# An attention block gated by an fp4 feed-forward on one core: another order of the first 90 microseconds

## The chip, the cores and the metric

The kernel runs on one core of one Trainium2 chip, as one launch. The metric is the device time of that core in microseconds. The five engines of the core run their own instruction streams in order: TensorE (matmuls and transposes), VectorE, ScalarE, GpSimd, and SyncE, which issues most of the DMAs. They wait for each other by semaphores.

## The reference, cut to what matters

The input `x` is 4 x 2048 x 256 in float32. It is normalized over the last axis, and the normalized tokens go two ways: through an attention without softmax (whose sums over all tokens reduce to the Gram matrix of the normalized tokens), and through a feed-forward of width 704 whose three products have both operands quantized to fp4 in blocks of 16.

```python
def fp4_quant_dequant(x):                    # blocks of 16 along the last axis
    scale = jnp.maximum(jnp.max(jnp.abs(xb), axis=-1, keepdims=True) / 6.0, 1e-12)
    xn = xb / scale
    q = _GRID[jnp.searchsorted(_MID, jnp.abs(xn))] * jnp.sign(xn) * scale
...
    h = jax.nn.silu(fp4_linear(x, w_gate)) * fp4_linear(x, w_up)
    return fp4_linear(h, w_down)
...
    xn = _layernorm(x, axis=-1)              # mean, variance, eps 1e-5
    s = attention(xn, Wq, bq, Wk, bk, Wv, bv, gamma)   # x + gamma * weight_value
    g = _silu(ffn(xn, w_gate, w_up, w_down))
    return x + s * g
```

The attention of a batch of 2048 tokens needs all tokens of that batch before any of its output can be made; the feed-forward of a group of tokens needs only that group and the weights.

## The kernel before, in words

The 8192 tokens are cut into 32 groups of 256, eight groups to a batch; a group is a tile of 128 partitions by two tokens by 256. Each group passes these stages, each a function of the kernel:

- `load_x`: the DMA of the tokens, issued by SyncE.
- `statistics` (lines 269 to 284): mean and variance by VectorE (`bn_stats`, `bn_aggr`), and two integer operations that start an inverse square root. `deviations` (286 to 298) ends that root by three Newton steps of four tiny operations each on GpSimd (`inv_sqrt_steps`, line 258) and makes `rstd` and `shift`.
- `normalize` (300): two ScalarE activations write the normalized tokens `xn`.
- `gram_step` (316): TensorE adds the group to the Gram matrix; `turn_xn` (336) transposes the group, evicted by ScalarE.
- `scale_x` (352) and `rounded` (229): the quantization to fp4. VectorE finds the largest of each block (line 151), its inverse (160, 162) and the quotient (177); ScalarE shortens it to 16 bits (`short`, 205); five VectorE operations round it to the grid and multiply by the scale (222 to 226, 235).
- `turn_xq` (360): TensorE transposes the quantized group, ScalarE evicts it.
- `gate_up` (436): a piece of the first two products: one of the group's two token halves with one of three chunks of the gate and up weights. ScalarE evicts it as `si` and `up`, GpSimd multiplies these to `h`. `pieces(n, i)` issues both halves of group n with chunk i.
- `scale_h`, `turn_q`, `rescale_h`: the quantization of `h`, with its transpose by DMA and its scales spread through memory. `down` (464) is the last product.

The weights pass the same quantization once: `scale_gu` (705) scales one of the three chunks (the quotient of chunks 1 and 2 is made by GpSimd, line 197), `turn_gu` transposes it, and `wd`, `turn_d` do the same for `w_down`, in six parts that a generator yields.

The order of instructions on each engine is the order in which these functions are called: the tile framework is put in a manual schedule and adds only the semaphores. Lines 776 to 879 are the front, a list of calls written out by hand, which quantizes the weights and brings groups 0 to 3 through gate and up and groups 4 to 6 partly; behind it a loop (893 to 966) handles one group per turn, with the steps of attention as a generator in between. `keep_busy` (496) issues matmuls of zeros whose result nobody reads.

PSUM buffers matter for the order: transposes rotate through two banks (`ps_tp`), gate-up pieces through two (`ps_gu`), so each needs ScalarE's eviction of the one before the last.

Of the kernel before, what the change touches and what calls it, by code (L numbers as in the profile page):

```python
# [15 lines left out]
LN_EPS = 1e-5  # L16
# [8 lines left out]
def kernel(  # L25
# [124 lines left out]
    def largest(sc: bass.AP, src: bass.AP):  # L150
        nc.vector.tensor_reduce(  # L151
            sc, src.rearrange("p a (n k) -> p a n k", k=BLK), AX.X, ALU.max, apply_absolute_value=True
        )
# [30 lines left out]
        )  # L184
        return sc, y, F, kind, nm

    def scaled(src: bass.AP, F: int, kind: str, nm: str, multiplier=nc.vector):
        n, a = F // BLK, src.shape[1]
        most = T * L if kind == "x" else HF
        sc = small.tile([P, most // BLK], F32, tag="scx" if kind == "x" else "sch", name=f"sc_{nm}")[:, 0:n]  # L190
        largest(sc, src)
        inv = inverse(sc, nm)
        if multiplier is nc.vector:
            return over(src, inv, F, kind, nm, sc)
        nc.vector.tensor_scalar(inv, inv, DOWN, None, ALU.mult)
        y = tok.tile([P, most], F32, tag="hqt", name=f"y_{nm}", bufs=2)[:, 0:F]
        multiplier.tensor_tensor(
            y.rearrange("p (a n k) -> p a n k", a=a, k=BLK),
            src.rearrange("p a (n k) -> p a n k", k=BLK),
            inv.rearrange("p (a n) -> p a n", a=a).unsqueeze(3).to_broadcast([P, a, n // a, BLK]),  # L200
            ALU.mult,
        )
        return sc, y, F, kind, nm

    def short(state):
        sc, y, F, kind, nm = state
        most = T * L if kind == "x" else HF
        t = tok.tile([P, most], F16, tag="tx" if kind == "x" else "th", name=f"t_{nm}", bufs=2)[:, 0:F]
        upper = y.bitcast(BF16).rearrange("p (f two) -> p f two", two=2)[:, :, 1]
        nc.scalar.activation(t, upper, AF.Copy, scale=1.0 + 2.0**-9)  # L210
        return t
# [17 lines left out]
    def rounded(state, t, multiplier=nc.vector) -> bass.AP:  # L229

        return rescaled(state, on_grid(state, t), multiplier)
# [16 lines left out]
    def inv_sqrt_first(v: bass.AP, nm: str):  # L248
        shape = list(v.shape)
        y = small.tile(shape, F32, tag=f"isq_y{shape}", name=f"isq_y_{nm}")  # L250
        r = small.tile(shape, F32, tag=f"isq_r{shape}", name=f"isq_r_{nm}")
        nc.vector.tensor_scalar(y.bitcast(I32), v.bitcast(I32), 1, None, ALU.logical_shift_right)
        nc.vector.tensor_scalar(
            y.bitcast(I32), y.bitcast(I32), -1.0, float(0x5F3759DF), ALU.mult, ALU.add
        )
        return y, r
# [12 lines left out]
    def statistics(*ns: int):  # L269

        ns = [n for n in ns if n < N]
        if not ns:
            return
        K = T * len(ns)
        mv = small.tile([P, 3 * T, 2], F32, tag="mv", name=f"mv_{ns[0]}")[:, 0:K, :]
        st = small.tile([P, 3 * T, 6], F32, tag="bn", name=f"bn_{ns[0]}", bufs=2)[:, 0:K, :]
        for i, n in enumerate(ns):
            for t in range(T):
                nc.vector.bn_stats(st[:, i * T + t, :], x_sb[n][:, t, :])
        for i in range(K):  # L280
            nc.vector.bn_aggr(mv[:, i, :], st[:, i, :])
        ve = small.tile([P, 3 * T], F32, tag="ve", name=f"ve_{ns[0]}", bufs=2)[:, 0:K]
        nc.vector.tensor_scalar(ve, mv[:, :, 1], LN_EPS, None, ALU.add)
        return ns, mv, ve, inv_sqrt_first(ve, f"ln{ns[0]}")

    def deviations(state):
        if state is None:
            return
        ns, mv, ve, first = state
        K = T * len(ns)  # L290
        rstd = small.tile([P, 3 * T], F32, tag="rstd", name=f"rstd_{ns[0]}")[:, 0:K]
        shift = small.tile([P, 3 * T], F32, tag="shift", name=f"shift_{ns[0]}")[:, 0:K]
        nc.gpsimd.tensor_scalar(shift, mv[:, :, 0], -1.0, None, ALU.mult)
        inv_sqrt_steps(rstd, ve, *first)
        nc.gpsimd.tensor_tensor(shift, shift, rstd, ALU.mult)  # L295
        for i, n in enumerate(ns):
            part = slice(i * T, (i + 1) * T)
            stats[n] = rstd[:, part], shift[:, part]

    def normalize(n: int):  # L300
        if n >= N:
            return
        rstd, shift = stats.pop(n)
        for t in range(T):
            nc.scalar.activation(  # L305
                xns[n % len(xns)][:, t, 0:L],
                x_sb[n][:, t, :],
                AF.Identity,
                scale=rstd[:, t : t + 1],
                bias=shift[:, t : t + 1],  # L310
            )
# [4 lines left out]
    def gram_step(n: int):  # L316

        if n >= N:
            return
        b, g = divmod(n, NG)  # L320
        if g == 0:
            grams[b] = ps_gr.tile([P, 512], F32, tag="gram", name=f"gram_{b}")
        xn = xns[n % len(xns)]

        for t in range(T):
            for c, o in ((0, 0), (1, L + 1)):
                nc.tensor.matmul(  # L327
                    grams[b][:, o : o + L + 1 - c * P],
                    xn[:, t, c * P : (c + 1) * P],
                    xn[:, t, c * P : L + 1],  # L330
                    start=(g == 0 and t == 0 and c == 0),
                    stop=(g == NG - 1 and t == T - 1),
                    skip_group_check=True,
                )
# [161 lines left out]
    def keep_busy(count: int):  # L496

        for _ in range(count):
            nc.tensor.matmul(opened["at"], zero[:, 0:P], zero, start=True, stop=True)

    def preset(n: int, pool=ps_at, tag: str = "at"):
        m_b = whole[n // NG][1]
        ready[n] = pool.tile([P, T, L], F32, tag=tag, name=f"at_{n}")
        nc.scalar.copy(ready[n], m_b.unsqueeze(1).to_broadcast([P, T, L]))
# [197 lines left out]

    wgu = const.tile([P, KC, NB * P], F32, tag="wgu", name="wgu")

    def scale_gu(i: int, multiplier):
        nb = chunks[i][1]
        return scaled(wgu_n[i][:, 0 : nb * L].unsqueeze(1), nb * L, "w", f"gu{i}", multiplier)

    def turn_gu(i: int, wz):
        j0, nb = chunks[i]  # L710
# [65 lines left out]
    open_bank(ps_at, "at")  # L776
    deviations(statistics(0))
    w0 = scale_gu(0, nc.vector)
    normalize(0)
    tw = short(w0)  # L780
    moments = statistics(1)
    s_x = scale_x(0)
    deviations(moments)
    tx = short(s_x)
    gram_step(0)
    turn_xn(0)
    keep_busy(9)
    wz = rounded(w0, tw)
    normalize(1)
    xz = rounded(s_x, tx)  # L790
    turn_gu(0, wz)
    turn_xq(0, xz)
    w1 = scale_gu(1, nc.gpsimd)
    s_x = scale_x(1)
    moments = statistics(2)
    gate_up(0, 0, *chunks[0])
    tx = short(s_x)
    tw = short(w1)
    gate_up(0, 1, *chunks[0])
    deviations(moments)  # L800
    gram_step(1)
    turn_xn(1)
    keep_busy(5)
    turn_xq(1, rounded(s_x, tx))
    w2 = scale_gu(2, nc.gpsimd)
    pieces(1, 0)
    wz = rounded(w1, tw)
    normalize(2)
    tw = short(w2)
    turn_gu(1, wz)  # L810
    moments = statistics(3)
    s_x = scale_x(2)
    deviations(moments)
    tx = short(s_x)
    gram_step(2)
    turn_xn(2)
    pieces(0, 1)
    wz = rounded(w2, tw)
    normalize(3)
    pieces(1, 1)  # L820
    turn_xq(2, rounded(s_x, tx))
    s_x = scale_x(3)
    tx = short(s_x)
    moments = statistics(4, 5, 6)
    pieces(2, 0)
    gram_step(3)
    turn_xn(3)
    xz = rounded(s_x, tx)
    deviations(moments)
    turn_gu(2, wz)  # L830
    wd = scaled(wd_n.unsqueeze(1), HF, "w", "d")
    pieces(2, 1)
    normalize(4)
    pieces(0, 2)
    td = short(wd)
    turn_xq(3, xz)
    s_x = scale_x(4)
    tx = short(s_x)
    pieces(1, 2)
    wdz = rounded(wd, td)  # L840
    turn_qk()
    wd_turns = turn_d(wdz)
    pieces(2, 2)
    load_x(7)
    load_x(8)
    h_state = scale_h(0)
    normalize(5)
    gate_up(3, 0, *chunks[0])
    next(wd_turns)
    gate_up(3, 1, *chunks[0])  # L850
    th = short(h_state)
    next(wd_turns)
    gram_step(4)
    turn_xn(4)
    turn_scales(0)
    turn_xq(4, rounded(s_x, tx))
    turn_q("h", 0, on_grid(h_state, th))
    gate_up(3, 0, *chunks[1])
    next(wd_turns)
    gate_up(3, 1, *chunks[1])  # L860
    next(wd_turns)
    h_state = 1, scale_h(1, 5)
    th = short(h_state[1])
    spread_biases()
    gate_up(3, 0, *chunks[2])
    next(wd_turns)
    gate_up(3, 1, *chunks[2])
    next(wd_turns)
    gram_step(5)
    s_x = scale_x_of(5, 1)  # L870
    tx = short(s_x)
# [188 lines left out]
```

## Time and profile before

| | |
|---|---|
| Median of 3 runs | 667.43 us (665.45 to 667.47) |
| Profiled execution | 666.58 us, span from first to last instruction 664.8 us |
| Busy in the span | PE 639.3 us, PEld 435.3, DVE 528.7, ACT 286.6, POOL 320.5 |
| Mean granted TensorE clock | 0.997 |
| First gate-up matmul of group 0 | 20.27 us |
| First gate-up matmul of group 4 (the loop) | 85.19 us |
| First gate-up matmul of group 5 | 101.68 us |

PE is TensorE's matmuls, PEld its weight loads (which overlap them), DVE is VectorE, ACT ScalarE, POOL GpSimd, SP SyncE. In a line of the timeline the first number is the start in us from the beginning of the span, the second the time to the end of the last of the instructions merged in it; then engine, line of the kernel, operation, output and input tiles with their shape, the count, and in brackets how long the engine had stood idle and what released it. In a list of waits the columns are: the operation that waited and the one that it waited for, total us, times, longest us. The chain that ended last is followed back from the last instruction to whatever released each step.

### The profile page before, as it was taken

Reading aid. Unit: us, or ns where it says so; the run is one execution under the profiler, and the core shown is the slowest. Engines: PE = TensorE matmul, PEld = TensorE weight load, DVE = VectorE, ACT = ScalarE, POOL = GpSimd, SP = SyncE. Lnnn points to the kernel's source line nnn. Section 1 sums busy time; section 2 is a strip of 40 time slices with the busy share of each in tenths; the row PEclk is TensorE's granted clock in tenths of the full one; section 3 lists DMA queues with packets and bytes.
Section 4 is the critical chain, followed back from the end, with each engine's and each line's share of the span. In section 5 each row is a group of like instructions: output and inputs, shape, how many; then the busy total and the mean of one; then the engine's idle time right before and its main releaser. Section 6 shows DMA issues by size and latency. Waiting matters only on the chain.

```text
span 664.8 us, 8117 instructions
## 1 busy us (share of the span) xinstructions
PE 639.3 (96%) x2486; PEld 435.3 (65%) x2486; DVE 528.7 (80%) x911; ACT 286.6 (43%) x701; POOL 320.5 (48%) x545
## 2 busy tenths in 40 slices
PE   3799999999999999999999999999999999999997
PEld 2446556656766666767666666766676666666886
DVE  6998997879866887867969786885997777888752
ACT  2366654344444444344453444444344444433230
POOL 5567445271635526264463636256263736537122
PEclk9999999999999999999999999999999999999999
DMA  9200488857489777764877888749778757884882
GB/s 228 77 17 0 54 101 138 117 53 85 103 122 140 140 115 108 127 99 119 137 112 101 135 125 130 120 121 141 84 113 126 111 113 114 120 125 72 150 176 97
DMA packets 86232, 74.19 MB, mean 112 GB/s; under 512 B 64076, under 2 KB 70444, under 8 KB 86188
## 3 DMA queue, kind: packets, MB, share of 16 engines
q1 hardware_dynamic: 85916, 73.40, 68.3%
q8 instruction: 20, 0.33, 0.2%
q10 hardware_dynamic: 272, 0.26, 0.1%
q14 instruction: 24, 0.20, 0.1%
HBM read 48.30 MB, written 10.27 MB: 88 GB/s over the span
## 4 chain that ended last, share of the span: by engine, by line
PE 83%; DVE 6%; POOL 3%; DMA 3%; ACT 2%; issue 1%; SPq 0%; DVEq 0%; ACTq 0%; POOLq 0%
PE gu L442 40%; PE dn L469 23%; PE at L511 8%; PE gram L327 5%; PE px L575 2%; PE tp_xn L344 2%; PE pm L661 1%; DMA qt_x<-t_x 1%; DMA wv_sb<-in_L_attn_Wv_dram 1%; DMA wgu_n<-in_L_ffn_w_gate_dram 1%; PE pa L640 1%; DMA x<-in_L_attn_x_dram 1%; POOL isq_r_ln L262 1%; PE tp_sc L396 0%; POOL h L455 0%
## 5 line engine op out<-in xcount | busy, mean ns | idle before, releaser
L442 PE MATMUL gu<-wgu,xqt 128*128 128x512 f32 (+1 forms) x768 | 315.9, 560 | 2.2 <-ACT xqt L314 2.2
L455 POOL TENSOR_TENSOR h<-si,up 128x256 f32<-128x256 f32 (+1 forms) x192 | 163.2, 857 | 274.4 <-ACT up L453 274.1
L442 PEld LDWEIGHTS gu<-wgu,xqt 128*128 128x128 f32 x768 | 143.0, 191 | 135.4 <-issue 105.4
L469 PE MATMUL dn<-wdt,hqt 128*128 128x256 f32 x768 | 171.0, 379 | 0.0
L469 PEld LDWEIGHTS dn<-wdt,hqt 128*128 128x128 f32 x768 | 144.2, 190 | 18.9
L451 ACT ACTIVATE si<-gu 128x256 f32<-128x256 f32 (+1 forms) x192 | 70.2, 366 | 192.2 <-PE gu L442 187.4
L419 DVE TENSOR_TENSOR xqt<-qt_x,se 128x512 f32<-128x512 bf16 x27 | 26.0, 961 | 72.0 <-DMA qt_x<-t_x 67.3
L453 ACT COPY up<-gu 128x256 f32<-128x256 f32 (+1 forms) x192 | 67.7, 353 | 0.0
L327 PEld LDWEIGHTS gram<-xn 128*128 128x128 f32 x256 | 44.0, 194 | 27.6 <-ACT xn L305 11.4
L511 PE MATMUL at<-M,xnt 128*128 128x256 f32 x256 | 59.7, 379 | 0.0
L429 DVE TENSOR_TENSOR hqt<-qt_h,se 128x1408 f32<-128x1408 bf16 x32 | 53.8, 1680 | 7.0 <-DMA qt_h<-t_h 7.0
L327 PE MATMUL gram<-xn 128*128 128x257 f32 (+1 forms) x256 | 48.9, 335 | 9.2 <-ACT xn L305 9.2
L177 DVE SCALAR_TENSOR_TENSOR y_h<-h,inv_h 128x1408 f32<-128x1408 f32 x32 | 54.7, 1711 | 2.5 <-ACT t_h L210 1.4
L210 ACT ACTIVATE t_h<-y_h 128x1408 f16<-128x1408 bf16 x32 | 44.3, 1385 | 17.5 <-DVE y_h L177 17.5
L151 DVE TENSOR_REDUCE scs<-h 128x88 f32<-128x1408 f32 x32 | 51.6, 1612 | 0.0
L511 PEld LDWEIGHTS at<-M,xnt 128*128 128x128 f32 x256 | 46.7, 190 | 6.7
L314 ACT COPY sct<-tp_sc 120x128 f32<-120x128 f32 (+1 forms) x32 | 8.4, 265 | 92.7 <-PE tp_sc L396 92.7
L305 ACT ACTIVATE xn<-x,shift,rstd 128x256 f32<-128x256 f32 x64 | 35.0, 597 | 28.2 <-POOL shift L295 28.2
L528 POOL TENSOR_TENSOR gate<-gate,xl 128x512 f32<-128x512 f32 x26 | 35.6, 1370 | 22.4 <-DVE gate L521 22.4
L225 DVE TENSOR_TENSOR t_h<-m_h,t_h 128x1408 bf16<-128x1408 bf16 x32 | 31.1, 972 | 1.1
L226 DVE TENSOR_TENSOR t_h<-t_h,m_h 128x1408 bf16<-128x1408 bf16 x32 | 28.5, 892 | 1.1
L164 DVE RECIPROCAL inv_h<-scs 128x120 f32<-128x120 f32 (+1 forms) x32 | 27.9, 873 | 1.1
(145 smaller groups left out, 662.9 us busy)
## 6 DMA issues: line engine op xcount, KB each, us to landing
se<-there SPq DMA_DIRECT2D x27, 960.0 KB
x<-in_L_attn_x_dram SPq DMA_DIRECT2D x32, 256.0 KB
out_dram<-gate SPq DMA_DIRECT2D x31, 256.0 KB
xl<-in_L_attn_x_dram SPq DMA_DIRECT2D x26, 256.0 KB
se<-there SPq DMA_DIRECT2D x5, 704.0 KB
there<-sct SPq DMA_DIRECT2D x27, 60.0 KB
wd_n<-in_L_ffn_w_down_dram SPq DMA_DIRECT2D x1, 704.0 KB
wgu_n<-in_L_ffn_w_up_dram SPq DMA_DIRECT2D x2, 256.0 KB
```

The costliest lines, as they stand in the source:

```text
L151: nc.vector.tensor_reduce(sc, src.rearrange("p a (n k) -> p a n k", k=BLK), AX.X, ALU.max, apply_absolute_value=True)
L177: nc.vector.scalar_tensor_tensor(y.rearrange("p (a n k) -> p a n k", a=a, k=BLK), src.rearrange("p a (n k) -> p a n k", k=BLK), DOWN, inv. ...
L210: nc.scalar.activation(t, upper, AF.Copy, scale=1.0 + 2.0**-9)
L327: nc.tensor.matmul(grams[b][:, o : o + L + 1 - c * P], xn[:, t, c * P : (c + 1) * P], xn[:, t, c * P : L + 1], start=(g == 0 and t == 0 an ...
L429: nc.vector.tensor_tensor(ht, turned.pop(("h", n)).rearrange("p g t -> p (g t)"), spread_sc[n][:, 0:NIC, :].rearrange("p g t -> p (g t)"), ...
L442: nc.tensor.matmul(gu[:, : nb * P], xqt[n][:, t, c, :], wgu[:, c, j0 * P : (j0 + nb) * P], start=(c == 0), stop=(c == KC - 1),)
L451: nc.scalar.activation(si[:, :nb, :], pair[:, :, 0, :], AF.Silu)
L453: nc.scalar.copy(up[:, :nb, :], pair[:, :, 1, :])
L455: nc.gpsimd.tensor_tensor(hs[n][:, o : o + nb * 64], si[:, :nb, :].rearrange("p j f -> p (j f)"), up[:, :nb, :].rearrange("p j f -> p (j f)"),
L469: nc.tensor.matmul(od[:, t, :], hqt[n][:, t * half + i, :], wdt[:, t * (half + 1) + i, :], start=(i == 0), stop=(i == half),)
L511: nc.tensor.matmul(ready[n][:, t, :], xt[:, c, t * P : (t + 1) * P], M[:, c, :], start=False, stop=(c == KC - 1), skip_group_check=True,)
L528: adder.tensor_tensor(gate, gate, x_last.pop(n), ALU.add)
```

## The change

The front is put in another order, and four things are new in it. The statistics of groups 1 to 3 are made by ScalarE (`sums`: two activations that sum the tokens, one tiny one for minus the mean, two that sum the squared differences), followed by `deviations_of`, which starts the root on VectorE, ends it on GpSimd and makes `shift` with one product. The largest of the blocks of the second weight chunk is found before group 0 is quantized, and its inverse directly behind group 0's quotient, with a `scaled` that takes a finished `sc`. The filler matmuls behind group 0 are eight of float32r with 256 columns and one of the old, and the second set of five is gone. `w_down` is scaled ahead of the tokens of group 3 and rounded ahead of them, and all pieces of groups 0 and 1 come before the pieces of group 2. `turn_qk` moves from behind group 1's last pieces to between two of its middle ones; the loads of groups 7 and 8 and the DMA transposes of group 0's `h` move too. The loop is unchanged.

```diff
-    def scaled(src: bass.AP, F: int, kind: str, nm: str, multiplier=nc.vector):
+    def largest_of(src: bass.AP, F: int, kind: str, nm: str) -> bass.AP:
+        most = T * L if kind == "x" else HF
+        sc = small.tile([P, most // BLK], F32, tag="scx" if kind == "x" else "sch", name=f"sc_{nm}")[:, 0 : F // BLK]
+        largest(sc, src)
+        return sc
+
+    def scaled(src: bass.AP, F: int, kind: str, nm: str, multiplier=nc.vector, sc=None):
...
+    def sums(n: int):
+        total = small.tile([P, T], F32, tag="total", name=f"total_{n}", bufs=2)
+        minus = small.tile([P, T], F32, tag="minus", name=f"minus_{n}", bufs=2)
+        square = small.tile([P, T], F32, tag="square", name=f"square_{n}", bufs=2)
+        xn = xns[n % len(xns)]
+        for t in range(T):
+            nc.scalar.activation(
+                xn[:, t, 0:L], x_sb[n][:, t, :], AF.Copy, accum_out=total[:, t : t + 1]
+            )
+        nc.scalar.activation(minus, total, AF.Copy, scale=-1.0 / L)
+        for t in range(T):
+            nc.scalar.activation(
+                xn[:, t, 0:L],
+                x_sb[n][:, t, :],
+                AF.Square,
+                bias=minus[:, t : t + 1],
+                accum_out=square[:, t : t + 1],
+            )
+        return n, minus, square
+
+    def deviations_of(state):
+        n, minus, square = state
+        ve = small.tile([P, T], F32, tag="ve1", name=f"ve1_{n}", bufs=2)
+        nc.vector.tensor_scalar(ve, square, 1.0 / L, LN_EPS, ALU.mult, ALU.add)
+        first = inv_sqrt_first(ve, f"ln{n}")
+        rstd = small.tile([P, T], F32, tag="rstd1", name=f"rstd1_{n}", bufs=2)
+        shift = small.tile([P, T], F32, tag="shift1", name=f"shift1_{n}", bufs=2)
+        inv_sqrt_steps(rstd, ve, *first)
+        nc.gpsimd.tensor_tensor(shift, minus, rstd, ALU.mult)
+        stats[n] = rstd, shift
...
+    def keep_busy_r(count: int):
+        z = zero.bitcast(mybir.dt.float32r)
+        for _ in range(count):
+            nc.tensor.matmul(opened["at"][:, 0:256], z[:, 0:P], z, start=True, stop=True)
```

The calls of the new front, down to the first call that stands where it did (the old ones are printed above):

```python
open_bank(ps_at, "at")
deviations(statistics(0))
w0 = scale_gu(0, nc.vector)
moments = sums(1)
sc1 = largest_gu(1)
normalize(0)
tw = short(w0)
deviations_of(moments)
s_x = scale_x(0)
w1 = scale_gu(1, nc.gpsimd, sc1)
tx = short(s_x)
gram_step(0)
turn_xn(0)
keep_busy_r(8)
keep_busy(1)
wz = rounded(w0, tw)
normalize(1)
gram_step(1)
moments = sums(2)
turn_xn(1)
xz = rounded(s_x, tx)
turn_gu(0, wz)
turn_xq(0, xz)
deviations_of(moments)
s_x = scale_x(1)
tw = short(w1)
tx = short(s_x)
gate_up(0, 0, *chunks[0])
normalize(2)
gate_up(0, 1, *chunks[0])
wz = rounded(w1, tw)
xz = rounded(s_x, tx)
gram_step(2)
turn_gu(1, wz)
turn_xn(2)
w2 = scale_gu(2, nc.gpsimd)
turn_xq(1, xz)
moments = sums(3)
gate_up(0, 0, *chunks[1])
s_x = scale_x(2)
tw = short(w2)
tx = short(s_x)
gate_up(0, 1, *chunks[1])
deviations_of(moments)
wz = rounded(w2, tw)
pieces(1, 0)
normalize(3)
gate_up(1, 0, *chunks[1])
turn_qk()
gate_up(1, 1, *chunks[1])
xz = rounded(s_x, tx)
gram_step(3)
turn_xn(3)
turn_gu(2, wz)
turn_xq(2, xz)
wd = scaled(wd_n.unsqueeze(1), HF, "w", "d")
s_x = scale_x(3)
gate_up(0, 0, *chunks[2])
td = short(wd)
gate_up(0, 1, *chunks[2])
tx = short(s_x)
pieces(1, 2)
wdz = rounded(wd, td)
xz = rounded(s_x, tx)
wd_turns = turn_d(wdz)
moments = statistics(4, 5, 6)
gate_up(2, 0, *chunks[0])
next(wd_turns)
gate_up(2, 1, *chunks[0])
next(wd_turns)
turn_xq(3, xz)
h_state = scale_h(0)
deviations(moments)
gate_up(2, 0, *chunks[1])
next(wd_turns)
gate_up(2, 1, *chunks[1])
next(wd_turns)
normalize(4)
gate_up(2, 0, *chunks[2])
next(wd_turns)
th = short(h_state)
gate_up(2, 1, *chunks[2])
load_x(7)
load_x(8)
next(wd_turns)
s_x = scale_x(4)
turn_q("h", 0, on_grid(h_state, th))
normalize(5)
gate_up(3, 0, *chunks[0])
tx = short(s_x)
turn_scales(0)
gate_up(3, 1, *chunks[0])
gram_step(4)
turn_xn(4)
turn_xq(4, rounded(s_x, tx))
pieces(3, 1)
h_state = 1, scale_h(1, 5)
th = short(h_state[1])
spread_biases()
pieces(3, 2)
gram_step(5)
```

## The prediction

> **What bounds the kernel now.** I read the page first (busy slices, the chain that ended last), then what TensorE waits for, then stretches of 10 us, then the timeline of the first 102 us.
>
> ```profile
> PE   3799999999999999999999999999999999999997
> ...
> DVE  6998997879866887867969786885997777888752
> ...
> PE 83%; DVE 6%; POOL 3%; DMA 3%; ACT 2%; issue 1%; SPq 0%; DVEq 0%; ACTq 0%; POOLq 0%
> ```
>
> From the third slice on TensorE is full, and it carries 83% of the chain. All that a new front can do is to let it begin its steady work earlier or later. The waits of TensorE over the whole run:
>
> ```profile
> PE gram L327 <- ACT xn L305: 9.2, 3, 8.0
> PE tp_xq L364 <- DVE y_x L235: 2.3, 2, 1.8
> PE gu L442 <- ACT xqt L314: 2.2, 3, 0.9
> ```
>
> They are nearly all in the front (behind 120 us three microseconds are left). The stretches (columns: length, then busy us and count of PE, PEld, DVE, ACT, POOL; clock, DMA share, GB/s):
>
> ```profile
> 10.00:20.00 10.00, 8.26 (x33) 5.57 (x33) 9.48 (x22) 5.66 (x10) 5.27 (x14) 1.00 1.01 291
> 20.00:30.00 10.00, 7.29 (x30) 4.20 (x31) 9.38 (x22) 4.04 (x9) 5.66 (x11) 1.00 0.02 9
> 30.00:40.00 10.00, 9.46 (x31) 5.16 (x32) 9.48 (x21) 4.64 (x11) 8.62 (x19) 0.83 0.12 29
> 40.00:50.00 10.00, 9.15 (x25) 4.22 (x24) 9.55 (x22) 5.78 (x15) 5.88 (x11) 1.00 0.00 0
> ```
>
> VectorE is as full as TensorE here and ScalarE half empty. The timeline (start, length):
>
> ```profile
> 11.21 0.19 POOL L260 TENSOR_TENSOR isq_r_ln<-isq_y_ln 128x2 f32<-128x2 f32 x1 [0.39 <-DVE isq_y_ln L253]
> ...
> 15.52 1.17 POOL L262 TENSOR_SCALAR isq_r_ln<-isq_r_ln 128x2 f32<-128x2 f32 x1
> ...
> 17.05 0.20 POOL L295 TENSOR_TENSOR shift<-shift,rstd 128x2 f32<-128x2 f32 x1
> ...
> 21.07 1.94 POOL L197 TENSOR_TENSOR y_gu<-wgu_n,inv_gu 128x1024 f32<-128x1024 f32 x1 [3.83 <-DVE inv_gu L195]
> ...
> 21.62 1.42 DVE L160 TENSOR_SCALAR sc_x<-sc_x 128x32 f32<-128x32 f32 x1
> ...
> 85.19 3.60 PE L442 MATMUL gu<-wgu,xqt 128*128 128x512 f32 x8
> ...
> 100.81 0.69 DVE L419 TENSOR_TENSOR xqt<-qt_x,se 128x512 f32<-128x512 bf16 x1 [2.05 <-DMA qt_x<-t_x]
> ...
> 101.68 3.64 PE L442 MATMUL gu<-wgu,xqt 128*128 128x512 f32 x8
> ```
>
> The inverse square root of one group takes GpSimd from 11.21 to 17.25 us, 6.0 us for 13 tiny operations, because VectorE's work blocks it. The loop's gate-up of group 4 starts at 85.19, that of group 5 at 101.68, 0.2 us behind its operand. These two are the finishing line: what comes after is unchanged and TensorE's. Operand 5 hangs on VectorE's last step for token group 5 (88.07 us) plus 13.4 us of transposes, so VectorE and TensorE must both come earlier for a gain.
>
> **The Trainium skill.** (1) "SBUF — State Buffer", section "SBUF: two separate sides": VectorE and GpSimd share a port pair as an exclusive lock, and the loser blocks for the whole instruction. The trace agrees: a VectorE scale of 0.18 us took 1.42 beside GpSimd's 1.94. (2) "TensorE: Matmul & The Clock Gate", "Part 1": after an idle window of about 3.4 us the array runs at half clock until a busy window has passed. Agrees: behind the gap of 26.8 to 29.9 us the clock was
>
> ```profile
> 30.00:31.00 1.00, 1.00 (x2) 0.52 0.03 8
> 31.00:32.00 1.00, 1.00 (x2) 0.50 0.00 0
> 32.00:33.00 1.00, 1.00 (x2) 0.50 0.00 0
> 33.00:34.00 1.00, 1.00 (x3) 0.78 0.00 0
> ```
>
> and gate-up records started 0.86 us apart instead of 0.43. Prices: "ScalarE: Activation LUTs", "What ACT_TABLE_LOAD costs".
>
> **The change, part by part.** Times of the new kernel are estimates, chained from durations in the timeline of before.
>
> *Removed.* VectorE loses bn_stats and bn_aggr of groups 1 to 3: 24.21 to 25.27 = 1.06 us each, 3.2 us. The second filler (1.24 us of TensorE) goes too; it lay in a gap.
>
> *Added on ScalarE*, which the trace doesn't show: per group two Copy and two Square of 128x256 with a sum, and one tiny operation. The page's price is 186 + 0.833 ns per element, 93 ns more per pointer, 93 ns of overlap (agrees: with two pointers 585, the trace has 599). So 2 x 0.31 + 0.19 + 0.40 + 0.49 = 1.7 us without the four reads of the sum. VectorE's such reads take 0.08 us, ScalarE's smallest instruction 0.20: with two waits on itself 2.2 to 2.7; I keep 1.7 as the lower end and take 2.25. The first set hides before 9.99 us, where ScalarE waits for shift 0, if x1 has landed by 7.7. The trace bounds that by 9.55, where VectorE reads it without a wait; of the 2.05 MB that come in the first 10 us (205 GB/s) it is complete at 1.05, so I take 7.5. If it came at 9.55, normalize 0 and step 1 would be 1.8 us later. Weights 1 likewise are read at 9.55 instead of 18.73; they are complete at 1.57 of the 2.05 MB, so I add no wait, and 0.5 us at the upper end. The other two sets stand ahead of evictions for which TensorE waits. The new filler (eight narrow matmuls) is 1.4 us at half the 0.35 us of the old ones, 3.5 us at most by the 0.43 us of a 256 column f32 product (24 records of dn in 5.18 us of the chain, two to a product); it hides until group 1 is normalized, and at worst until ScalarE is free at 20.0.
>
> *Step 1, to the first gate-up.* VectorE from 9.55: largest of weights 1, 1.25; start of root 1, 0.6; scale x0, 1.93; inverse of weights 1, 1.0; weights 0 rounded, 3.51: 17.9 (before 16.56). GpSimd is through with root 1 at 16.8 (5.3 us: more of it lies beside reductions and reciprocals) and has y_gu1 queued: it gets the lock at 17.9 and holds it 1.7 us (0, if it fell on reductions; 1.94 at most, its length). x0 rounded (2.17) ends at 21.8, before 18.73. ScalarE: normalize 1 to 17.7, sums 2 to 20.0, xnt, two wgu with a bank wait between them 22.1, xqt 23.1. First gate-up 23.2, before 20.27: 2.9 late.
>
> *Step 2, to weights 1.* Root 2 starts at 21.8 + 0.6 and takes the 6.0 us shown, the neighbours being the same: 28.5. Normalize 2 stands ahead of ScalarE's further evictions; TensorE has nothing from 26.7 to 29.2. Then normalize 1.1, si and up 0.65, transposes and wgu to 32.3, xnt 33.05, xqt 33.65. Gate-up (0, chunk 1) at 32.8.
>
> *Step 3, to w_down.* Sums 3 to 35.9; si, up 0.65; t_gu 0.85; t_x 0.65; si, up 0.65; product on GpSimd 0.75: 39.45. Root 3 is queued behind that product and beside dense VectorE work, 5.2 us (before 37.44 to 42.81): 44.7. Behind it on ScalarE normalize 1.1, si, up 0.65, two wqkt 1.15, si, up 0.65, xnt 0.6, the last wgu: 49.95. Gate-up (0, chunk 2) starts at 50.0. Before, the same TensorE work was done at 53.58 - 3.44 (piece 2,0) + 0.87 (turn_qk) = 51.0: 1.0 us gained. Then 1.3 + 0.2 + 0.65, and the 1.4 us of t_d: 53.6.
>
> *Step 4, to the loop.* VectorE has scaled w_down and x3 by 49.5 and waits 4.1 us for t_d, which stands in ScalarE's queue behind step 3. w_down rounded 5.3 (5.06 in before): 58.9, TensorE waiting since 57.3. x3 2.4, statistics 4 to 6 3.15, scale h0 4.2: 68.65. The root of 4 to 6 blocks on y_h, as in before (1.67 us): shift at 69.15, normalize 70.25, eviction and t_h to 72.9, grid h0 3.1: 76.0; t_x at 76.65 behind normalize 5; x4 rounded 78.85. TensorE then has 0.44 + 3.44 + 2.58 + 1.31 + 0.44 + 0.1 = 8.3 us to gate-up 4: **87.2, before 85.19: +2.0**. On VectorE h1 and x5 end at 90.0 (88.07), so operand 5 comes at 103.4 and TensorE wants it at 103.7: both agree.
>
> Moved at no cost: turn_qk (0.87 us of the same TensorE queue); the loads of x 7 and 8 and qt_h ahead of there and se on SP, as SP has nothing else until 86 us and se is read at 90.
>
> Sum: span 664.8 + 2.0 = 666.8; with the 1.8 around it (666.58 against 664.8) 668.6; the median of the runs is 0.85 above the profiled one: **669.5**, +0.31%. A measurement of this kernel tells about 0.3% (2 us) from no change.
>
> **Rivals.**
> *A, the roots run free (faster).* Alone a root takes 3.5 us (13 steps of 0.27, as from 5.42 us). If VectorE stands waiting when roots 2 and 3 run, they end 2.5 and 1.7 us earlier, all of step 4 moves up 4.2, and gate-up 4 starts at 83.0: 665.3; TensorE's own floor from w_down on (24.2 us behind 54.7) would allow more, so to 663. It decides from 4 us saved on the two. For: ScalarE is late in my chain, which empties VectorE. Against: the 6.0, 6.4 and 5.4 us of before.
> *B, VectorE sets the pace (same).* Its 3.2 us saved pay for the new waits if these are 4 instead of 7 us (t_d 4.1, then x4, h0, ve3, w2): 85.2 and 667.4. For: it is 94% busy in before. Against: behind the wait for shift 3, t_d has a dozen ScalarE instructions ahead of it.
> *C, the clock falls again (slower).* The thin stretch of 26.7 to 32.8 has a quarter of a window busy; before, a fifth sufficed to lose the clock. 3.4 us at half clock: +1.7, 671.2.
>
> **How the numbers follow.** Forecast 0.33 (own range 668 to 671.5), C 0.15, B 0.30, A 0.22. Low end 663.5 from A with sums of 1.7 us, high end 673 from C with sums of 2.7 us twice on the path. Slower 0.48, same 0.30, faster 0.22.
>
> **What would show it.** First gate-up near 23.2 us; root 2 to about 28.5 and root 3 to 44.7; ScalarE waiting some 2.5 and 3.5 us for shift 2 and 3; the w_down grid starting near 53.6 after a VectorE gap of some 4 us; gate-up 4 at 87.2 and 5 at 103.7. A gate-up 4 before 84 makes it wrong, as does a sum set under 1.5 us.

## The result and the profile after

The changed kernel takes 670.44 us (median of 6 runs, 669.57 to 672.84) against 666.76 of the kernel before (6 runs): ratio 1.0056, 95% interval 1.0039 to 1.0074, so 3.7 us slower. The profiled execution took 671.93 us with a span of 670.1 (before: 666.58 and 664.8).

The page of the kernel after, its busy slices, the granted clock by slice and the shares of the chain that ended last:

```profile
PE   3698899999999999999999999999999999999997
...
DVE  6988889687967898786978787795996867788753
...
PEclk9898999999999999999999999999999999999999
...
PE 80%; DVE 7%; POOL 6%; ACT 3%; issue 2%; DMA 2%; SPq 0%; DVEq 0%; ACTq 0%; POOLq 0%
```

From the sixth slice on TensorE is as full as before. The difference lies in the first five: the second has 6 instead of 7, the fourth and fifth 8 instead of 9, and in two slices the clock was not fully granted. In the chain GpSimd has 6% instead of 3% and TensorE 80% instead of 83%. What TensorE waits for, over the whole run:

```profile
PE gram L365 <- ACT xn L343: 13.0, 6, 7.8
PE tp_xq L402 <- DVE y_x L241: 2.4, 1, 2.4
PE tp_d L785 <- DVE y_d L241: 2.0, 1, 2.0
```

The Gram matrices wait 13.0 us for normalized tokens instead of 9.2, and there are two single waits of 2.0 and 2.4 us, one for w_down and one for x4. Stretches of 10 us (length, busy us and count of PE, PEld, DVE, ACT, POOL; clock, DMA share, GB/s):

```profile
30.00:40.00 10.00, 9.81 (x36) 6.01 (x34) 7.03 (x16) 7.07 (x22) 3.22 (x3) 0.83 0.12 29
...
60.00:70.00 10.00, 9.85 (x35) 5.46 (x36) 9.66 (x25) 4.84 (x14) 5.37 (x15) 0.83 0.00 0
...
80.00:90.00 10.00, 8.92 (x25) 5.01 (x26) 7.46 (x10) 4.07 (x11) 2.69 (x4) 0.83 0.40 97
```

The kernel before had one row with a clock of 0.83, this one has three. TensorE is busy for 8.9 to 9.9 us of each of them: at half clock it needs longer for the same matmuls (eight gate-up matmuls took 3.70 us at full clock and 5.40 us mostly at half clock in the kernel before, at 20.27 and 29.87), and a full row hides it. The timeline (start, length, and in brackets the idle time ahead with what ended it):

```profile
7.96 0.19 ACT L299 ACTIVATION_READ_ACCUMULATOR xn<-x 128x1 f32 x1
...
17.06 2.99 DVE L241 TENSOR_TENSOR y_gu<-t_gu,sc_gu 128x1024 f32<-128x1024 bf16 x1
...
28.92 1.09 ACT L343 ACTIVATE xn<-x,shift,rstd 128x256 f32<-128x256 f32 x2 [2.58 <-POOL shift L321]
...
46.43 1.10 ACT L343 ACTIVATE xn<-x,shift,rstd 128x256 f32<-128x256 f32 x2 [3.52 <-POOL shift L321]
...
91.11 3.60 PE L480 MATMUL gu<-wgu,xqt 128*128 128x512 f32 x8
...
107.60 3.60 PE L480 MATMUL gu<-wgu,xqt 128*128 128x512 f32 x8
...
111.58 1.58 PE L365 MATMUL gram<-xn 128*128 128x257 f32 x8 [0.38 <-ACT xn L343]
```

Gate-up n is the first gate-up matmul of group n. Gate-up 4 starts at 91.11 us (before 85.19), gate-up 5 at 107.60 (101.68), both 5.9 us late. The last row is the Gram matrix of group 7 (Gram 7 below), the first work of the loop behind gate-up 5; before, it started at 105.16:

```profile
105.16 1.52 PE L327 MATMUL gram<-xn 128*128 128x257 f32 x8
```

Of all kernels profiled in this study, 14 with the two above, the time from that row to the end of the span lies between 558.3 and 560.7 us. So the question of every run below is: when does Gram 7 start?

### The profile page after: what moved, and what is told of

It is laid out like the page before. It is cut to its first block, busy times and chain, and to the rows that moved or that the text cites. A ratio compares the mean times of both kernels' runs of the same rounds, so it can differ in the third digit from the quotient of the medians.

```text
span 670.1 us, 8124 instructions
## 1 busy us (share of the span) xinstructions
PE 641.8 (96%) x2481; PEld 437.1 (65%) x2481; DVE 525.3 (78%) x899; ACT 293.0 (44%) x728; POOL 318.9 (48%) x542
## 4 chain that ended last, share of the span: by engine, by line
PE 80%; DVE 7%; POOL 6%; ACT 3%; issue 2%; DMA 2%; SPq 0%; DVEq 0%; ACTq 0%; POOLq 0%
PE gu L480 37%; PE dn L507 22%; PE at L555 8%; PE gram L365 5%; PE px L619 2%; PE tp_xn L382 2%; PE pm L705 1%; DMA qt_x<-t_x 1%; POOL isq_r_ln L267 1%; POOL isq_r_ln L268 1%; DMA wgu_n<-in_L_ffn_w_up_dram 1%; POOL isq_r_ln L266 1%; PE pa L684 1%; POOL isq_y_ln L269 1%; ACT xn L343 1%
## 5 line engine op out<-in xcount | busy, mean ns | idle before, releaser
L231 DVE TENSOR_TENSOR t_h<-m_h,t_h 128x1408 bf16<-128x1408 bf16 x32 | 28.8, 901 | 1.1
```

## The experiments

Ratios are against runs of the kernel before on the same chip, whose median lay between 666.0 and 666.9 us.

| kernel | median us | ratio, 95% interval | gate-up 4 | Gram 7 | mean granted clock of its runs |
|---|---|---|---|---|---|
| before | 666.76 | 1 | 85.19 | 105.16 | 0.9959 |
| after | 670.44 | 1.0056 (1.0039 to 1.0074) | 91.11 | 111.58 | 0.9937 |
| fill | 668.83 | 1.0026 (1.0016 to 1.0036) | 86.59 | 107.28 | 0.9984 |
| dve | 671.89 | 1.0078 (1.0060 to 1.0095) | 91.26 | 111.19 | 0.9905 |
| bsums | 669.28 | 1.0031 (1.0015 to 1.0047) | 88.94 | 108.88 | 0.9947 |
| bfill | 666.38 | 0.9994 (0.9982 to 1.0006) | 87.28 | 107.29 | 0.9978 |
| early | 667.50 | 1.0007 (0.9993 to 1.0021) | 85.33 | 107.45 | 0.9948 |
| bearly | 665.02 | 0.9962 (0.9948 to 0.9976) | 84.31 | 104.38 | 0.9973 |
| bjoint | 667.81 | 1.0009 (0.9996 to 1.0021) | 87.21 | 107.29 | 0.9949 |
| wdlate | 673.33 | 1.0101 (1.0082 to 1.0120) | 91.47 | 111.49 | 0.9920 |
| wdlate2 | 673.96 | 1.0105 (1.0084 to 1.0126) | 92.88 | 113.00 | 0.9928 |
| w1late | 672.75 | 1.0099 (1.0081 to 1.0116) | 91.33 | 111.58 | 0.9924 |
| earlytail | 669.19 | 1.0043 (1.0029 to 1.0058) | 87.22 | 107.36 | 0.9938 |
| earlyfill | 667.54 | 1.0015 (1.0002 to 1.0027) | 85.77 | 108.00 | 0.9981 |

Each kernel has 5 to 22 runs; before has 6 in the first columns and 46 (those beside fill) in the last, and 0.9964 to 0.9977 on the other chips. Gate-up 4 and Gram 7 are from one profiled run each, which need not be a typical one: that of fill was the fastest of 22 (667.42 us, 1.4 below the median), those of after, dve, bsums, early, bfill, bjoint and earlyfill lie 1.1 to 2.0 us above their medians. The weights of chunk 0 were first read at 6.00 us in fill and at 6.98 in early, and what follows moves with them. A clock of 0.9937 over 669 us is 4.2 us of full clock missed (of the 6.0 us of the profiled run, at 0.991, some 0.8 lie at the very end, with a clock of 0.92 from 660 to 670 us).

**Theory and rivals.** Below, sums n, root n and shift n are the sums, the inverse square root and the shift of group n, and x n its tokens. The theory at the start: the changed kernel is late because statistics as ScalarE work stand in a queue behind the previous root, and because each wait of TensorE lets the clock fall. Rivals: the sums' own time on ScalarE; weights 1 in front of everything, with the lock between VectorE and GpSimd; the new order of w_down.

### fill: the clock alone

```diff
+    keep_busy(8)
     gram_step(2)
...
     gate_up(2, 0, *chunks[0])
+    keep_busy(8)
     next(wd_turns)
...
     turn_xn(4)
+    keep_busy(9)
     turn_xq(4, rounded(s_x, tx))
```

> The changed kernel, with zero matmuls added to TensorE's queue in the three places where it waited over 2 us (8 of them ahead of the Gram matrix of group 2, 8 behind the first gate-up of group 2, 9 ahead of the last transposes of group 4). Theory 1, the clock: the half-clock stretches behind the waits of 2.20 and 2.38 us are on the path. Without the first, everything up to the w_down grid comes 1.7 us earlier, without the last another 1.9 us; the middle one (60 to 64 us) is covered by VectorE. Gate-up 4 at 87.5 us instead of 91.1, gate-up (0, chunk 1) at 33.1 instead of 34.9, granted clock 1.00 in every 10 us row, time 666.8 (666 to 668). Theory 2, the lower clock only fills time in which TensorE would have waited for VectorE and ScalarE: the rows show 1.00 too, but gate-up 4 stays within 0.7 us of 91.1 and the time at 670 to 671.

Measured 668.83 us. The two rows of 10 us of fill that answer to the last two of after:

```profile
60.00:70.00 10.00, 8.60 (x39) 4.99 (x37) 7.73 (x21) 5.60 (x16) 6.37 (x18) 1.00 0.00 0
80.00:90.00 10.00, 10.00 (x35) 5.74 (x34) 9.38 (x13) 6.46 (x16) 4.47 (x6) 1.00 0.31 78
```

The clock stays at 1.00, and gate-up 4 comes at 86.59. This run began 1.0 us sooner (its first gate-up 22.67 against 23.67), so 3.5 us of the 4.5 are the fillers' work, against 3.6 expected. Between the medians the gain is only 2.0 us (ratio 1.0026 against 1.0056): the two profiled runs lie further apart than their kernels, and in fill gate-up 5 waits 0.5 us for its operand, so behind there VectorE takes back some of the gain. The clock that fill still missed on average, 1.1 us, doesn't explain the difference: its 13 runs with a clock of 0.999 or more have a median of 668.89. The clock is a cause: theory 1 holds in its mechanism, for about half of the 3.7 us, and its range of 666 to 668 was missed.

### dve and bsums: the order without the sums, the sums without the order

```diff
-    moments = sums(1)
+    moments = statistics(1)
...
-    deviations_of(moments)
+    deviations(moments)
```

(dve; the same for groups 2 and 3.)

> The changed kernel with the statistics of groups 1 to 3 back on VectorE; the new order of weights and w_down stays. Theory 1, the new order and the clock make the kernel slower and the sums on ScalarE help a little: VectorE does 1.06 us more three times, the first two on the path to the first gate-up and to root 2, the third saves about 1 us of its wait for the sums: 671.5 us (670.5 to 673.5), first gate-up at 24.5 to 25. Rival, the sums are what makes it slower, because they stand ahead of evictions in ScalarE's queue: without them 667.5 to 669, and gate-up 4 before 89.5.

bsums is the kernel before with sums and deviations_of in place of statistics and deviations, sums of group 1 ahead of normalize(0), those of groups 2 and 3 where VectorE's statistics were called. In statistics VectorE also starts the root; now deviations_of does, so that for group 3 this start moves behind the scaling of group 2.

> The kernel before with only one part of the change: the statistics of groups 1 to 3 by ScalarE, in the places where VectorE computed them. Theory 1 (the sums help, the order loses): VectorE, 94% busy, gets 3.2 us back and ScalarE has room, so gate-up 4 comes 1 to 2.5 us ahead of 85.2: 664.5 to 666. Rival (the sums lose): ScalarE's queue is late by 2.3 us twice, 668 to 669.5. If TensorE sets the pace in the kernel before: 666.8, no change.

dve took 671.89 us, as theory 1 had it (671.5): with VectorE doing the statistics the new order is slower than the old one by 0.78%. Its interval overlaps that of after, so whether the sums help in that order isn't settled; in its profiled run the clock was 0.55 from 20 to 30 us, behind waits of 2.49 and 2.69 us ahead of the first gate-up. bsums took 669.28: theory 1 fell there, the rival's number came. Sums alone, in the old order, cost 0.31%, 2.1 us. Timeline of bsums around group 3, ScalarE's first sum, GpSimd's first step of root 3, ScalarE's normalizing:

```profile
37.68 0.44 ACT L293 ACTIVATE xn<-x 128x256 f32<-128x256 f32 x1
...
40.65 0.23 POOL L260 TENSOR_TENSOR isq_r_ln<-isq_y_ln 128x2 f32<-128x2 f32 x1 [4.60 <-DVE isq_y_ln L253]
...
46.57 1.09 ACT L337 ACTIVATE xn<-x,shift,rstd 128x256 f32<-128x256 f32 x2 [4.37 <-POOL shift L315]
```

In the kernel before, VectorE read x3 at 33.70, ahead of the tokens of group 2, for which it had to wait anyway. As ScalarE work the same statistics stand behind the normalizing of group 2 and three instructions more: they begin at 37.68, root 3 at 40.65 instead of 37.44, and group 3 is normalized 3.6 us later (46.57 against 42.98). VectorE was through with the scaling of group 2 at 38.62 and waited 1.38 us more for the sums; the rest of the 3.2 us comes from the root's start behind that scaling. So both places in the queues count, that of the sums and that of the root's start; bearly moves both.

### bearly: the same sums, called sooner

```diff
     s_x = scale_x(0)
+    moments2 = sums(2)
     tx = short(s_x)
     gram_step(0)
     turn_xn(0)
+    moments3 = sums(3)
...
-    s_x = scale_x(2)
     deviations_of(moments3)
+    s_x = scale_x(2)
```

(against bsums; its own calls of sums for groups 2 and 3 go. The last two lines put the start of root 3 back ahead of the scaling of group 2.)

> The kernel before with only the statistics of groups 1 to 3 by ScalarE, and those of groups 2 and 3 early (in ScalarE's idle time ahead of the normalizing of group 1); the roots start where they did. Theory 1 (the serial chain was what made the sums lose in the kernel before, where they cost 2.1 us): root 3 starts no later than in the kernel before, VectorE keeps its 2 to 3 us, gate-up 4 at 83 to 84.5 and 664.7 to 666.3. Rival (the sums' time on ScalarE is what costs): 668 to 669.5, as with the sums in VectorE's places. If nothing in this stretch hangs on VectorE: 666.9.

Measured 665.02 us, 0.38% below the kernel before and within the range of theory 1. Root 3 now ends with this row, at 41.67 (42.81 before, 46.53 in bsums):

```profile
41.48 0.19 POOL L315 TENSOR_TENSOR shift<-minus,rstd 128x2 f32<-128x2 f32 x1
```

The instructions are those of bsums; only their places differ, and these are worth 4.3 us between the two medians. The two parts, the early sums and the start of root 3, weren't run apart. This version beats both kernels.

### early: sums and roots sooner in the changed kernel

```diff
     s_x = scale_x(0)
+    moments2 = sums(2)
     w1 = scale_gu(1, nc.gpsimd, sc1)
...
     turn_xn(0)
+    moments3 = sums(3)
...
     wz = rounded(w0, tw)
+    deviations_of(moments2)
...
     turn_xq(0, xz)
-    deviations_of(moments)
+    deviations_of(moments3)
```

(the old calls of sums for groups 2 and 3 and of deviations_of for group 3 go.)

> The changed kernel with the sums of groups 2 and 3 taken out of the queue behind the roots: ScalarE computes them as soon as the tokens are there (group 2 ahead of its short copy of x0, group 3 behind the copy of the transposed group 0), and roots 2 and 3 are started directly behind the rounding of weights 0 and of x0. Theory 1 (a serial chain: sums n+1 stand behind the normalizing of n, which waits for root n, so root n+1 can't start before root n is through): shift 2 at 26.5 to 27 us instead of 28.9, shift 3 near 33 instead of 46.4, no wait of ScalarE for shift 3, gate-up (0, chunk 1) near 32.3, gate-up 4 at 86 to 88, 666 to 668. Rival (the rounding of weights and tokens on VectorE with the lock, and the order of w_down, set the pace whatever the roots do): gate-up 4 within 1 us of 91.1 and 669.5 to 670.5.

Measured 667.50 us (theory 666 to 668), 2.9 us below after and not to be told from the kernel before. Shift 3 is there 14 us sooner:

```profile
31.80 0.19 POOL L321 TENSOR_TENSOR shift<-minus,rstd 128x2 f32<-128x2 f32 x1
...
106.80 1.09 ACT L343 ACTIVATE xn<-x,shift,rstd 128x256 f32<-128x256 f32 x2 [4.01 <-POOL shift L333]
107.45 1.58 PE L365 MATMUL gram<-xn 128*128 128x257 f32 x8 [2.03 <-ACT xn L343]
```

Gate-up 4 starts at 85.33 and gate-up 5 at 101.83, as in the kernel before. The mean clock is nearly that of after (0.9948, 0.9937), so the gain is not the clock's.

It doesn't show the serial chain of theory 1, though, as the roots were moved as well as the sums. In after, VectorE started root 2 straight behind the rounding of x0, without a wait, and root 3 with a wait of 1.43 us for the sums; GpSimd then took up root 3 only 2.6 us after its operand was there (38.41), behind two products `h`:

```profile
22.14 0.16 DVE L316 TENSOR_SCALAR ve<-square 128x2 f32<-128x2 f32 x1
...
37.84 0.17 DVE L316 TENSOR_SCALAR ve<-square 128x2 f32<-128x2 f32 x1 [1.43 <-ACT xn L304]
...
41.00 0.51 POOL L266 TENSOR_TENSOR isq_r_ln<-isq_y_ln 128x2 f32<-128x2 f32 x1
```

And dve, where VectorE makes the statistics and no sums stand in ScalarE's queue, has shift 3 no sooner than after (46.20 there), with the operand of root 3 there at 37.02:

```profile
46.59 0.19 POOL L333 TENSOR_TENSOR shift<-shift,rstd 128x2 f32<-128x2 f32 x1
```

So root 3 is late in the changed order because it is called late; that the sums stand behind the last root is not needed for it.

The first of the three rows of early above is shift 3. The other two rows show where the rest stays: the root of groups 7 and 8, beside dense VectorE work from 99 to 106.8 us, is late next, and Gram 7 waits 2.0 us for it in this run, the slowest of 14 (before: 105.16, TensorE without a wait).

### bfill: the clock in the kernel before

```diff
-    keep_busy(5)
+    keep_busy(14)
```

> The kernel before with its second row of zero matmuls lengthened from 5 to 14, so that TensorE does not stand idle from 26.8 to 29.9 us. If the clock that is lost there in the kernel before is on its path: granted clock 1.00 in the row from 30 to 40, gate-up 4 at 83.5 instead of 85.2, 665.1 us. If VectorE sets its pace from there on: gate-up 4 at 85.2 and 666.8.

Measured 666.38 us, no change. Of the two answers the first falls: gate-up 4 did not come earlier but at 87.28, in a profiled run 2.0 us above the median. The row from 30 to 40 us has a clock of 1.00 (before 0.83), but the same gate-up pair of group 2 that took 3.70 us before took longer here:

```profile
47.63 5.40 PE L442 MATMUL gu<-wgu,xqt 128*128 128x512 f32 x8 [0.68 <-ACT xqt L314]
```

With its clock kept, TensorE ran ahead, waited again (1.01 us for x2, 0.90 for an eviction) and lost the clock there. The filler only moved the loss, and it brought nothing, as the next operands were not ready sooner.

### w1late: weights 1 behind the rounding of x0

```diff
-    sc1 = largest_gu(1)
...
-    w1 = scale_gu(1, nc.gpsimd, sc1)
...
     turn_xq(0, xz)
+    w1 = scale_gu(1, nc.gpsimd)
     deviations_of(moments)
```

> The changed kernel with one part undone: largest value, inverse and GpSimd product of weights 1 stand behind the rounding of x0, as in the kernel before, instead of ahead of the rounding of weights 0. Theory 1 (the serial chain of sums and roots and the lost clock pace the front; weights 1 early cost 2 to 3 us to the first gate-up, but root 2 is then held up by the product): first gate-up 2.5 to 3.5 us earlier, shift 2 only 0.5 to 1 us earlier, gate-up (0, chunk 1) 1.5 us earlier at most, 668.5 to 670.5. Rival (weights 1 in front of everything, with the lock, are what makes the kernel slower): gate-up 4 2.5 to 4 us earlier and 666 to 668.

Measured 672.75 us, 2.3 us slower than after, with intervals that don't meet. The first gate-up came at 20.91, 2.8 us sooner as expected, but it was not the path:

```profile
30.38 2.94 PE L365 MATMUL gram<-xn 128*128 128x257 f32 x8 [5.77 <-ACT xn L343]
```

GpSimd now has the product of weights 1 (21.40 to 23.33) ahead of root 2, shift 2 ends at 29.70 instead of 28.88, and TensorE, sooner through with the first gate-up, waits 5.77 us instead of 2.20 and loses its clock. So the rival, weights 1 in front of everything, falls: quantizing them early is a gain in this order, although it brings the lock with it (VectorE's 2.99 us at 17.06, where the same operation alone takes 1.22). What the lock costs by itself wasn't run.

### wdlate, wdlate2, earlytail: the w_down order undone

```diff
-    wd = scaled(wd_n.unsqueeze(1), HF, "w", "d")
     s_x = scale_x(3)
+    wd = scaled(wd_n.unsqueeze(1), HF, "w", "d")
...
-    wdz = rounded(wd, td)
     xz = rounded(s_x, tx)
+    moments = statistics(4, 5, 6)
+    turn_xq(3, xz)
+    deviations(moments)
+    wdz = rounded(wd, td)
```

(and from pieces(2, 0) on the calls of the kernel before; in wdlate normalize(4) stands between two pieces of group 2.)

> The changed kernel up to the tokens of group 3, and from there the order of the kernel before: tokens of group 3 ahead of w_down, the w_down transposes between the gate-ups of group 3 instead of those of group 2. Theory 1 (the w_down order costs, because TensorE waits 2.05 us for w_down and 2.38 us for x4 and loses its clock behind each): no wait over 1 us behind 50 us, gate-up 4 at 83.5 to 86, 665 to 667. Rival (the loss is all in the front, before 51 us; the w_down order only moves waits): gate-up 4 within 1 us of 91.1, 669.5 to 670.5.

> As the run wdlate, with its fault mended: normalizing group 4 stands behind all evictions of group 2's gate-ups in ScalarE's queue, not between them, where it held TensorE up for 6.7 us. Theory 1 (the w_down order costs by the waits for w_down and x4): TensorE waits under 1 us behind 55 us, gate-up 4 at 84 to 87, 665.5 to 668. Rival (the loss of the changed kernel is made before 51 us, the w_down order is neutral): 669.5 to 671. If the old order suits only the old front: over 671.

> The run early (sums of groups 2 and 3 ahead of the roots) with the tail of wdlate2 (tokens of group 3 ahead of w_down). Theory 1 (the serial chain and the w_down order are two separate losses and their cures add): gate-up 4 at 81 to 84, 662.5 to 665, faster than both kernels. Rival (VectorE sets the tail's pace whichever order it works in): as early, 667 to 668.

All three missed: 673.33, 673.96 and 669.19 us, the last to be held against early's 667.50. In wdlate the eviction of a gate-up stood behind normalize(4), and TensorE waited 6.7 us:

```profile
69.51 6.23 PE L480 MATMUL gu<-wgu,xqt 128*128 128x384 f32 x12 [6.71 <-ACT up L491]
```

With that mended (wdlate2) the wait is 2.3 us, but x4 is still late: the root of groups 4 to 6 runs beside the rounding of w_down and takes from 59.93 to 67.26, 7.3 us, where the kernel before had started it at 52.58, ahead of w_down. So nothing shows the w_down order to cost anything; undone in this way the kernels lose 2.9, 3.5 and (against early) 1.7 us. This is no exact return to the old tail, in which the statistics of groups 4 to 6 came before w_down was scaled; such a kernel wasn't run.

### bjoint and earlyfill: two attempts at more

bjoint is bearly with one root for groups 2 and 3 together, started behind the rounding of weights 0, and Gram 2 in the place of two zero matmuls.

> The kernel before with early sums by ScalarE for groups 2 and 3, one common root for both (four columns instead of two, started behind the rounding of weights 0), and the Gram matrix of group 2 moved into the gap ahead of the transposes of x1 in place of two of the five zero matmuls. Theory 1 (the roots and what waits for them pace the front): ScalarE waits for no shift after the first two, the gap of 3.1 us of TensorE shrinks to under 1.5 us, no clock is lost in 30 to 34 us, gate-up 4 at 80 to 82.5, 662.5 to 665, faster than both kernels. Rival (VectorE's scaling and rounding of w_down, x3, x4 and h0 set the finishing line): gate-up 4 at 84 to 85.5, 665.7 to 667.

Measured 667.81 us, neither faster than the kernel before nor than bearly. The common root was through at 22.66 us, as meant, but VectorE waited 0.74 us for the sums ahead of the rounding of x0, and that is where TensorE waited:

```profile
20.52 0.63 PE L404 MATMUL tp_xq<-ident,y_x 128*128 128x128 f32 x4 [2.36 <-DVE y_x L235]
21.83 5.40 PE L482 MATMUL gu<-wgu,xqt 128*128 128x512 f32 x8 [0.68 <-ACT xqt L354]
```

One late operand early on and the clock is gone for the first gate-up (5.40 us instead of 3.70); it fell again at 39 us behind a wait of 2.11. Three things were changed at once here, so this run doesn't show what starting root 2 sooner is worth by itself.

earlyfill is early with zero matmuls ahead of Gram 1 (6), the first w_down transposes (8) and the transposes of x4 (9).

> The run early with zero matmuls in TensorE's queue ahead of the Gram matrix of group 1 (6, where it waited 2.44 us and lost its clock), ahead of the first transposes of w_down (8) and ahead of the transposes of x4 (9). Theory 1 (the serial chain and the lost clock are two losses whose cures add): granted clock 1.00 in every row from 10 us on, gate-up 4 0.5 to 2 us earlier than in early (85.3), 665.3 to 666.7. Rival (early has already taken the whole gain, and its remaining waits are VectorE's): gate-up 4 within 0.5 us of 85.3, 667 to 668.

Measured 667.54 us: the rival. The clock is 1.00 throughout, yet gate-up 4 stays at 85.8 and Gram 7 comes at 108.00, behind a wait of 2.13 us for the root of groups 7 and 8. The two cures don't add: in this profiled run that root is the finishing line, and TensorE's clock ahead of it is spare. Read the other way round, fill and earlyfill both hold the clock and differ only by 1.3 us, with intervals that overlap (1.0016 to 1.0036, 1.0002 to 1.0027): with the clock held, the gain of the sooner sums and roots isn't clear of noise.

## Why the prediction was right, and where it was off

The range of 663.5 to 673 held the time and slower was the likeliest side. The point forecast of 669.5 is 0.9 us low. That it is so near is in part luck: it started from 667.43, the median of three runs, and six runs of the same kernel gave 666.76. The forecast difference was 2.1 us, the measured one 3.7. The steps of the forecast, with fill as the kernel in which the clock doesn't fall (fill's times moved by the 1.0 us that it began sooner):

| step | forecast | after | fill + 1.0 |
|---|---|---|---|
| first gate-up | 23.2 | 23.67 | 23.67 |
| root 2 ends | 28.5 | 28.88 | 28.88 |
| gate-up (0, chunk 1) | 32.8 | 34.86 | 33.24 |
| root 3 ends | 44.7 | 46.40 | 44.79 |
| gate-up (0, chunk 2) | 50.0 | 50.98 | 49.38 |
| shift of groups 4 to 6 | 69.15 | 71.18 | 69.35 |
| gate-up 4 | 87.2 | 91.11 | 87.59 |
| gate-up 5 | 103.7 | 107.60 | 104.78 |

- *Sums set, 2.25 us.* Right: 7.64 to 9.91, 2.27 us. The part without a price was the read of the sum, 0.19 us for each of four. The first gate-up was 0.5 us later than forecast because weights 0 landed later in this run (read at 6.87 us instead of 6.34).
- *Lock of weights 1, 1.7 us.* Right in size (2.99 against 1.22 us), one instruction sooner than forecast: it fell on the last step of the rounding of weights 0, not on the rounding of x0.
- *Roots blocked, 6.0 and 5.2 us.* Right: 6.1 (22.79 to 28.88) and 5.4 us (41.00 to 46.40), and for the reasons given: root 2 started behind the rounding of x0, root 3 behind a product on GpSimd. ScalarE waited 2.58 and 3.52 us for the two shifts, forecast 2.5 and 3.5. Rival A (roots run free) is out.
- *VectorE's wait for t_d, 4.1 us.* It was 2.65: sums 3 had kept VectorE waiting already (1.43 us at 37.84), and its x3 was scaled later. The rounding began at 54.38 (53.6), so the path was right.
- *Rival B (VectorE paces, no loss).* Out: VectorE was busy only 7.0 to 7.5 us of 10 in four stretches of the front (30 to 40, 50 to 60 and 70 to 90 us).
- *"Sum: span 664.8 + 2.0."* This is the step that failed, as a term mis-sized. Rival C, kept out of the sum with a chance of 0.15 and 1.7 us, came true, and not once but three times in the profiled run, at 30, 61 and 82 us: the waits of 2.05 and 2.38 us for w_down and x4, which the forecast itself contained (TensorE waiting from 57.3 to 58.9), were not asked what they do to the clock. The first and the last were on the path, together 3.5 us at gate-up 4, as fill shows. Between the medians the clock is worth 2.0 us, which leaves 1.9 us over the kernel before (668.83 against 666.91), close to the 2.0 us of the forecast's sum. So the path was right and the term for the clock, put at nothing, was the error. What makes the other 1.9 us is not isolated by a run: early points to the places of sums and roots, but earlyfill against fill leaves this within the noise, and the new fillers behind group 0, the move of `turn_qk` and the moved loads were not undone one by one.

The forecast took for the clock gate a gap of 26.8 to 29.9 us in the kernel before. The trace has two waits of TensorE there, of 1.77 and 0.68 us, with the transposes of x1 between them; so waits of this size had cost the clock already, and those of 2.0 and 2.4 us were to be asked the same. Whether such a wait does cost it depends on the run (last section), so three losses in one run are also chance.

What the forecast didn't ask is where the loss could have been avoided. It took the places of sums and roots as given. early and bearly show that with both called sooner the whole change is no slower than the kernel before (1.0007, 0.9993 to 1.0021), and the sums in the old order are 0.38% faster.

## What to carry to other kernels

Work that is moved to an idle engine takes on that engine's queue: before pricing the instruction, list what stands ahead of it there and what that waits for, try work that depends on a load alone at the first idle stretch, not only where the old engine had it, and start what hangs on it (here the roots) early in its own queues too. Ask of every forecast wait of TensorE of about 2 us what it may do to the clock (here: is TensorE busy for less than half of some 3.41 us), and expect a filler to pay only where TensorE, and not the next operand, sets the pace. When a gain doesn't arrive, look for the finishing line that is next, as Gram 7 behind gate-up 5 was in the profiled runs of early and earlyfill.

## What the runs showed of the hardware

In the profiled run of after TensorE lost its clock behind waits of 2.20, 2.05 and 2.38 us, shorter than the idle window of about 3.4 us that the Trainium skill gives ("TensorE: Matmul & The Clock Gate", "Part 1"). The length of the wait alone doesn't decide: a wait of 2.20 us ahead of Gram 2 lost the clock in after and not in wdlate, and early's waits of 2.05 and 2.39 us cost none. The page says that the window runs freely, not from the kernel's start, and the traces agree. From rows of half a microsecond, the losses of after begin at 30.14, 60.86 and 81.34 us and last 3.41 us each (1.7 us of full clock; the row from 30 to 31 has 0.57, the next three 0.50, 0.50 and 0.72). The distances between the beginnings, 30.72 and 20.48 us, are 9 and 6 times 3.413. The six other kernels with more than one loss (dve, bsums, bjoint, wdlate2, w1late, earlytail) keep to whole multiples too, and two longer losses last two and three times as long (6.8 us in wdlate, 10.2 in dve).

Cut into windows of 3.413 us on this grid, from 13 to 115 us, each of the 20 losses begins behind a window in which TensorE was busy for at most 0.51 of the time; the three of after had 1.21, 1.36 and 1.03 us of 3.41. No window with more was followed by a loss, and six between 0.42 and 0.51 weren't either. So here the measurement differs from the page: the window need not be idle. The wait of 2.20 us lay within one window in after (26.73 to 30.14) and was cut by the grid at 28.53 in wdlate, with 1.74 and 2.66 us busy on its two sides. Where the grid lies changes from run to run, and so does what a wait of 2 us costs.

Runs of one kernel differ therefore, but not by the clock alone. The 46 runs of the kernel before took 664.75 to 669.51 us with clocks from 0.993 to 1.000; the twelve slowest (from 668.53) had at most 0.996, the seven with 0.999 or more took 665.60 to 667.14. The 13 runs of fill with 0.999 or more still spread from 667.42 to 669.96, which these records don't explain.
